# Stage 1 of a folded weight chain: six one-tap products in place of seven blocks, three middle taps evicted by VectorE, and the next stage's shared products in the same PSUM tile

## The chip, the cores and the metric

One core of one Trainium2 chip. The metric is device time in microseconds (us) of one execution. Before the change three runs gave 475.52, 476.29 and 476.63 us; the median is 476.29 us. All arithmetic is fp32.

## The reference

A residual block on `x` of shape (128 samples, 64 channels, 1024 positions). Each sample has its own style vector, and four modulated convolutions with three taps follow one another:

```
out = x
for typ in ('same', 'upsample', 'same', 'downsample'):
    s = style @ mw.T + mb                       # per sample and input channel
    weight = SCALE * w * s[:, None, :, None]    # per sample
    weight *= rsqrt(sum(weight**2 over inputs and taps) + 1e-8)
    same:       out = conv(out, weight, pad 1) + b
    upsample:   out = blur(conv_transpose(out, weight, stride 2) + b)
    downsample: out = conv(blur(out), weight, stride 2) + b
return x + out
```

There is no nonlinearity between the layers. So for each sample the four convolutions and the blurs are one linear map, and away from the ends of the row it is one short filter per pair of channels.

## The kernel before

**What it computes per group.** Samples are handled in 32 groups `q` of four. Two samples share a 128-partition tile (64 channels each), so each group has two "columns" `r` of a weight chain. For every group the kernel first multiplies the four layers' weights together, as 64x64 matrices, in three stages, and then applies the combined filter to the data.

- `scale3` (ScalarE) scales the last layer's three taps by the group's style into `wd`. With it come the sums of neighbouring taps, since `wd` is scaled from `w3x`, which holds the three taps and two sums.
- Stage 1 (`stage1`, or its two halves `stage1_a` and `stage1_b`) multiplies layer 3's taps `wd` by layer 2's taps. A product of two three-tap filters has five taps. The split version forms them from products of taps and of sums of taps, as in the multiplication of polynomials with fewer products. It writes PSUM tile `psS`. ScalarE evicts it with a scale into the SBUF tile `S` (line 399), and VectorE finishes two taps from the sums (line 481). GpSimd adds one slot (line 484).
- Stage 2 (`stage2`) multiplies the five taps `S` by the nine blurred taps `E` of the upsampling layer, into PSUM tile `psR` (line 506, or line 589 in the plain form). For groups 8 to 30 the work is shared: `share_sums` (VectorE, line 501) adds two pairs of slots of `S`, `share` multiplies these by `E` (three products, line 506), `share_copy` (ScalarE, line 529) spreads the two results over four blocks of `psR`, and `stage2_rest` adds the other products to them.
- Stage 3 multiplies by the first layer's taps (line 621) and gives the combined filter `Wf`; `combine_a` and `combine_b` form its sums `H` on VectorE (line 712).
- `conv0` to `conv4` (line 803) apply it to the data planes; each of the five is 12 matmuls of 340 columns, in three groups of four 64x64 quadrants. `output` (ScalarE, line 880) scales the results and SyncE's queue stores them.

**PSUM.** The pool `ps_w` has one buffer: two tiles `u0` and `u1`, one bank each (512 fp32 columns), one for each column `r`. `psS`, `psR` and `psW` follow one another in it. A new tile in it waits until the last reader of the old one is done. `psA` (two buffers of two banks) and `Y` (two banks, all the time) hold the results of the convolutions in columns 0 to 339. Columns from 344 on are used for small things: in `psA`, `share` puts its products there; in `Y`, the constants of the bias path.

**Order.** The schedule is written out by hand (`tc.manual_schedule()`), so every engine runs its instructions in the order of the program text, and the tile framework adds only the semaphores. In the steady state `turn_of(q)` handles the last convolutions of group `q`, the middle of group `n = q+1`, stages 2 and 3 of group `c = q+2` and stage 1 of group `s = q+4`. Its order on TensorE is `stage2(c)`, `conv2(q)`, `stage3_b`, `conv4(q)`, `stage3_a`, `conv3(n)`, `stage1_a(s)`, `conv0(q)`, `stage1_b(s)`, `share(c+1)`, sometimes a small job at the ends of the rows (`slot`), `conv1(n)`. `sharing(q)` holds for q = 5 to 27, which is 23 turns. The first turns (`early_turn`, q = 0 to 3) have the same parts in another order and no `share`. The split stage 1 runs for 28 groups, the plain `stage1` for groups 0, 1, 2 and 6.

VectorE's order around the place is: `in04` (line 790), `share_sums` (line 501), `in_g2` (line 712 on 684 columns), in most turns a small job of the bias and row-end path (`SIDE`), then the pair of line 481, then `in_g01` (line 712 on 1376 columns). ScalarE's is: `output(q, 2)`, the two evictions of `stage1_a`, `copy_m3` (line 842), `output(q, 1)`, `share_copy`, `output(q, 0)`, `scale3`.

The main line of `stage1_b` and `share` in a turn is

```
        conv0(q, *((2,) if entry else range(K)))
        ...
        outputs(q, 1)
        if s < NQ:
            stage1_b(s)
        in_g01(c)
        if sharing(q):
            share(c + 1, banks(q))
            share_copy(c + 1)
        outputs(q, 0)
        ...
        conv1(n, *((2,) if entry else range(K)))
```

Of the kernel before, what the change touches and what calls it, by code (L numbers as in the profile page):

```python
# [48 lines left out]
F32 = mybir.dt.float32  # L49
AF = mybir.ActivationFunctionType  # L50
ALU = mybir.AluOpType
# [3 lines left out]
C = 64  # L55
K = 3
# [7 lines left out]
def kernel(  # L64
# [326 lines left out]


    w3 = wio[3]
    Wq = {}
    chain = {}

# [4 lines left out]
            eng.tensor_scalar(dst, src, f, None, op0=ALU.mult)  # L401


    w3x = const.tile([P, 5, C], F32, name="w3x")
    w2n = const.tile([P, 5, C], F32, name="w2n")

    def split_weights():
        nc_g.tensor_copy(w3x[:, :K], w3)
        nc_g.tensor_scalar_mul(w2n[:, :K], woi[2], -1.0)
        for t, src in ((w3x, w3), (w2n, woi[2])):  # L410
            nc_g.tensor_add(t[:, K:], src[:, : K - 1], src[:, 1:])

    DIRECT = 3

    def scale3(q, engs=(nc_a, nc_a)):
        wd = []
        src = w3 if q < DIRECT else w3x
        n = src.shape[1]
        for j in range(2):
            t = wd_pool.tile([P, 5, C], F32, tag="wd", name=f"wd{q}_{j}")  # L420
            scaled_copy(engs[j], t[:, :n], src, tA[:, q, j : j + 1])
            wd.append(t)
        chain[q] = wd
# [17 lines left out]
    def flat(t):  # L441
        return t.rearrange("c a o -> c (a o)")

    EVEN = slice(0, K, 2)

    def stage1(q, pool=None, engs=(nc_a, nc_a), between=None):

        wd = chain[q]
        ps = unit(pool or ps_w, f"psS{q}")
        for k, (at, at1) in enumerate(((0, 3), (3, 1), (1, 4))):  # L450
            tap_matmul(ps, wd, at, 2, woi[2][:, k, :], EVEN, first=k == 0)
            tap_matmul(ps, wd, at1, 1, woi[2][:, k, :], slice(1, 2), last=k == K - 1)
        if between:
            between()
        st, _ = s_tiles(q)
        for r in range(2):
            scaled_copy(engs[r], flat(st[r][:, 1:6]), ps[r][:, : 5 * C], tB[:, q, r : r + 1])
        chain[q] = st
        return ps

    def stage1_a(q, ps=None):

        ps = ps or unit(ps_w, f"psS{q}")
        wd = chain[q]
        tap_matmul(ps, wd, 2, 2, w2n[:, 0, :], EVEN, first=True)
        tap_matmul(ps, wd, 3, 2, w2n[:, 2, :], EVEN)
        tap_matmul(ps, wd, 1, 1, w2n[:, 1, :], slice(1, 2))
        st, t = s_tiles(q)
        for r in range(2):
            scaled_copy(nc_a, flat(st[r][:, :4]), ps[r][:, C : 5 * C], tBn[:, q, r : r + 1])  # L470
        chain[q] = wd, ps, st, t

    def stage1_b(q):

        wd, ps, st, t = chain[q]
        tap_matmul(ps, wd, 2, 1, w2n[:, 3, :], slice(3, 4))
        tap_matmul(ps, wd, 4, 1, w2n[:, 4, :], slice(4, 5), last=True)
        for r in range(2):
            p1 = st[r][:, 0:1, :].to_broadcast([P, 2, C])
            sums = ps[r][:, 2 * C : 6 * C].rearrange("c (a b o) -> c a b o", a=2, b=2)[:, :, 0]  # L480
            nc_v.scalar_tensor_tensor(
                st[r][:, 4:6, :], sums, tB[:, q, r : r + 1], p1, op0=ALU.mult, op1=ALU.subtract
            )
        nc_g.tensor_add(t[:, :, 2], t[:, :, 2], t[:, :, 0])  # L484
        chain[q] = st
        whole[q] = t

    whole, shared_ps = {}, {}
    later = wsq.rearrange("c l k o -> c (l k) o")
# [8 lines left out]

    def share_sums(q):
        t = whole[q]  # L500
        nc_v.tensor_add(t[:, :, 6:8], t[:, :, 1:5:3], t[:, :, 2:6:3])

    def chain_matmul(dst, weight, st, slots, last=False):
        for r, rows in enumerate(HALF):
# [9 lines left out]

    def share(q, ps):

        at = [NB + 4 + i * C for i in range(3)]
        p12, p34 = ([b[:, i:j] for b in ps] for i, j in zip(at, at[1:]))
        chain_matmul(p12, E[:, 2], chain[q], slice(6, 7))
        chain_matmul(p34, E[:, 6], chain[q], slice(6, 7))  # L520
        chain_matmul(p34, E[:, 5], chain[q], slice(7, 8), True)
        shared_ps[q] = [b[:, at[0] : at[2]] for b in ps]

    def share_copy(q):

        ps = unit(ps_w, f"psR{q}")
        for r in range(2):
            src = shared_ps[q][r].rearrange("c (a o) -> c a o", a=2)
            nc_a.copy(  # L529
                ps[r][:, C : 5 * C].rearrange("c (a b o) -> c a b o", a=2, b=2),  # L530
                src[:, :, None, :].to_broadcast([P, 2, 2, C]),
            )
        shared_ps[q] = ps

    def stage2_rest(q):

        ps = shared_ps.pop(q)
        block = lambda i, n=1: [b[:, i * C : (i + n) * C] for b in ps]
        apart = [b[:, : 4 * C].rearrange("c (a b o) -> c a b o", a=2, b=2)[:, :, 0] for b in ps]
        plan = (  # L540
            (apart, E[:, 0], slice(1, 4, 2)),
            (block(1), Ed[:, 0], slice(2, 3)),
            (block(2), Ed[:, 1], slice(1, 2)),
            (block(3), E[:, 2], slice(3, 4)),
            (block(3), Ed[:, 2], slice(2, 3)),
            (block(4), Ed[:, 3], slice(1, 2)),
            (block(4), E[:, 4], slice(3, 4)),
            (block(5, 2), E[:, 8], slice(2, 4)),
            (block(5), E[:, 6], slice(3, 4)),
            (block(1, 2), E[:, 1], slice(4, 6)),  # L550
            (block(2), E[:, 3], slice(4, 5)),
            (block(3), Ed[:, 4], slice(5, 6)),
            (block(4), Ed[:, 5], slice(4, 5)),
            (block(5), E[:, 7], slice(5, 6)),
        )
        for n, (dst, weight, slots) in enumerate(plan):
            chain_matmul(dst, weight, chain[q], slots, n == len(plan) - 1)
        return ps
# [18 lines left out]
    def stage2_taps(q, taps, ps):  # L577

        st = chain[q]
        for n in taps:  # L580
            e = n - 2
            if e % 2 == 0:
                a, lo, m = slice(1, 4), e // 2 + 1, 3
            else:
                a, lo, m = slice(4, 6), (e + 3) // 2, 2
            for r, rows in enumerate(HALF):
                for c, cols in enumerate(HALF):
                    src = st[c if r == 0 else 1 - c]
                    nc.tensor.matmul(  # L589
                        ps[r][cols, lo * C : (lo + m) * C],  # L590
                        E[rows, e + 2, :],
                        src[rows, a, :],
                        start=(n == 0),
                        stop=(n == 8),
                        skip_group_check=True,
                    )
        return ps
# [885 lines left out]
    def turn_of(q):  # L1483
        n, c, s = q + 1, q + 2, q + 4
        entry = q == FIRST
        stage2(c)
        if entry:
            sum2(q)
            conv4(q)
            combine_a(n)  # L1490
            r_sums(c, nc_v)
        else:
            conv2(q)
            r_sums(c, nc_g)
            sum2(q)
            in2(n, nc_g)
        side(TABLES, q)
        for i in range(3):
            load(c + 1, slice(i, i + 1))
        stage3_b(c, open_a(n))  # L1500
        if entry:
            conv0(q, 0, 1)
        else:
            combine_a(n)
            conv4(q)
        stage3_a(c)
        combine_b(n)
        conv3(n)
        if entry:
            copy_m3(n)  # L1510
            stage1_a(s)
        outputs(q, 2)
        if not entry:
            if s < NQ:
                stage1_a(s)
            copy_m3(n)
        in04(n)
        if sharing(q):
            share_sums(c + 1)
        in_g2(c)  # L1520
        side(SIDE, q)
        if q in SMALL:
            l, bs = SMALL[q]
            nc_v.memset(high(bs.stop - bs.start), 0.0)
        conv0(q, *((2,) if entry else range(K)))
        if entry:
            conv1(n, 0, 1)
        outputs(q, 1)
        if s < NQ:
            stage1_b(s)  # L1530
        in_g01(c)
        if sharing(q):
            share(c + 1, banks(q))
            share_copy(c + 1)
        outputs(q, 0)
        if q in SLOTS:
            matmuls, width, rest = SLOTS[q]
            slot(matmuls, width, Y_banks)
            rest()
        if s == NQ:  # L1540
            slot(ends3, 3, unit(ps_w, "psE"), 3)
            rest3()
        conv1(n, *((2,) if entry else range(K)))
        if q in SMALL:
            small(q)
        sum1(n)
        in3(c)
        side(LATE, q)
        if s == NQ:
            in04(c)  # L1550
        in1(c, nc_g)
        if s + 1 < NQ:
            scale3(s + 1)
# [168 lines left out]
```

## Time and profile before

| | |
|---|---|
| runs | 475.52, 476.29, 476.63 us, median 476.29 |
| profiled execution | span 475.5 us from the first to the last instruction, beside 475.52 us of the fastest run shown; the page gives no other time for it |
| TensorE (PE) | busy 469.7 us, 99% |
| TensorE weight loads (PEld) | 349.5 us, 74%, beside the matmuls |
| VectorE (DVE) | 417.3 us, 88% |
| ScalarE (ACT) | 312.0 us, 66% |
| GpSimd (POOL) | 165.8 us, 35% |
| granted TensorE clock | 0.998 |

A row of the groups' view reads: line, engine, operation, tile written and tiles read, shape, count, then busy time in us and the mean duration of one in ns, then the idle time of the engine before it and what ended it. A row of the timeline reads: start and extent in us, engine, line, operation, tiles, shape and count of merged instructions; in square brackets stands the idle time just before and its releaser. Each fp32 matmul appears as two records, so a product of one 64x64 block over both columns and both halves (four quadrants) is eight records.

### The profile page before, as it was taken

What the parts mean: (1) busy time and instruction counts of PE and PEld (TensorE: products, weight loads), DVE (VectorE), ACT (ScalarE), POOL (GpSimd) and SP (SyncE); (2) the same over time, 40 slices, a digit from 0 to 9 for tenths busy, and PEclk for the clock granted to TensorE, in tenths of its full rate; (3) what the DMA queues carried; (4) which work ended last, traced back from release to release, by engine and by line L of the source; (5) the groups of instructions that cost most, each with busy time, mean ns of one, the idle gap of its engine ahead of it and who ended that gap; (6) DMA issues with size and microseconds to landing.
All of it is one profiled execution on the core that took longest, in us unless ns stands there. A gap on an engine that the chain in (4) does not pass through costs nothing.

```text
span 475.5 us, 26771 instructions
## 1 busy us (share of the span) xinstructions
PE 469.7 (99%) x11932; PEld 349.5 (74%) x11932; DVE 417.3 (88%) x694; ACT 312.0 (66%) x711; POOL 165.8 (35%) x200
## 2 busy tenths in 40 slices
PE   9999999999999999999999999999999999999996
PEld 6987788777678876677776677766788787876653
DVE  3889998879989998899979899979998999999896
ACT  4565657577766676766667666667666777766464
POOL 3634033664444342233432233422333423243200
PEclk9999999999999999999999999999999999999999
DMA  5237456535445554345544454543555544455225
GB/s 176 71 115 224 150 151 180 152 113 177 139 145 166 166 166 136 123 150 169 163 150 126 130 168 152 178 124 121 152 164 169 164 145 147 148 152 161 80 91 193
DMA packets 52707, 70.71 MB, mean 149 GB/s; under 512 B 6000, under 2 KB 50672, under 8 KB 52592
## 3 DMA queue, kind: packets, MB, share of 16 engines
q1 hardware_dynamic: 52368, 68.78, 46.3%
q8 instruction: 93, 1.52, 1.4%
q10 hardware_dynamic: 224, 0.22, 0.1%
q14 instruction: 22, 0.18, 0.1%
HBM read 35.36 MB, written 33.62 MB: 145 GB/s over the span
## 4 chain that ended last, share of the span: by engine, by line
PE 99%; DVE 0%; ACT 0%; issue 0%
PE psA L803 47%; PE Y L803 12%; PE psR L506 9%; PE psW L621 7%; PE psA L621 7%; PE psS L428 6%; PE psR L589 5%; PE psA L506 2%; PE Y L1044 2%; PE Y L183 1%; PE Y L379 1%; PE psM L220 0%; PE psE L1044 0%; PE Y L255 0%; DVE o L882 0%; PE psM L255 0%
## 5 line engine op out<-in xcount | busy, mean ns | idle before, releaser
L803 PE MATMUL psA<-T,H 64*64 64x340 f32 x2304 | 185.9, 446 | 0.0
L803 PEld LDWEIGHTS psA<-T,H 64*64 64x64 f32 x2304 | 90.7, 133 | 46.9 <-issue 2.5
L712 DVE SCALAR_TENSOR_TENSOR G<-X 128x1376 f32<-128x1376 f32 (+2 forms) x65 | 78.0, 1206 | 0.2
L776 POOL TENSOR_TENSOR T<-G 128x684 f32<-128x684 f32 x28 | 46.3, 1652 | 73.7 <-DVE G L712 73.7
L484 POOL TENSOR_TENSOR S<-S 128x128 f32<-128x128 f32 x28 | 21.6, 772 | 139.7 <-ACT S L399 139.6
L399 ACT ACTIVATE R<-psR,tC 128x448 f32<-128x448 f32 x63 | 36.6, 631 | 43.6 <-PE psR L506 25.8
L803 PE MATMUL psA<-T,Wf 64*64 64x340 f32 x768 | 63.7, 446 | 0.0
L803 PE MATMUL Y<-T,Wf 64*64 64x340 f32 x768 | 62.4, 451 | 0.0
L712 DVE SCALAR_TENSOR_TENSOR Y<-m,psA 128x340 f32<-128x340 f32 x62 | 32.0, 516 | 28.2 <-PE psA L803 26.9
L399 ACT ACTIVATE psW<-psA 128x128 f32<-128x128 f32 x100 | 19.3, 268 | 49.1 <-PE psA L621 45.0
L790 DVE TENSOR_TENSOR T<-G 128x1368 f32<-128x1368 f32 (+1 forms) x33 | 50.8, 1541 | 0.0
L399 ACT ACTIVATE Wf<-psW,t 128x256 f32<-128x256 f32 (+2 forms) x76 | 32.7, 480 | 26.7 <-PE psW L621 26.4
L761 DVE TENSOR_TENSOR T<-X 128x684 f32<-128x684 f32 x32 | 47.7, 1492 | 0.0
L506 PE MATMUL psR<-S,E 64*64 64x64 f32 (+1 forms) x1472 | 46.8, 237 | 0.0
L781 POOL TENSOR_TENSOR T<-G 128x684 f32<-128x684 f32 x28 | 46.5, 1660 | 0.0
L428 PEld LDWEIGHTS psS<-wd,w2n 64*64 64x64 f32 x1120 | 35.1, 133 | 12.9 <-issue 0.3
L506 PEld LDWEIGHTS psR<-S,E 64*64 64x64 f32 x1472 | 39.5, 134 | 4.9 <-ACT psR L529 0.2
L803 PEld LDWEIGHTS Y<-T,Wf 64*64 64x64 f32 x768 | 30.3, 132 | 16.8
L803 PEld LDWEIGHTS psA<-T,Wf 64*64 64x64 f32 x768 | 29.8, 133 | 14.5
L880 ACT ACTIVATE o<-psA,tb,td 128x340 f32<-128x340 f32 x63 | 37.1, 648 | 5.0 <-PE psA L803 2.8
L880 ACT ACTIVATE o<-y,tb,td 128x340 f32<-128x340 f32 x62 | 38.5, 678 | 0.0
L880 ACT ACTIVATE o<-Y,tb,td 128x340 f32<-128x340 f32 x62 | 36.1, 639 | 2.8 <-PE Y L803 2.0
(180 smaller groups left out, 840.4 us busy)
## 6 DMA issues: line engine op xcount, KB each, us to landing
out<-o SPq DMA_DIRECT2D x191, 170.0 KB, 2.6
X<-in_x SPq DMA_DIRECT2D x150, 172.0 KB, 3.4
X<-in_x SPq DMA_DIRECT2D x14, 516.0 KB, 5.0
par<-in_params SPq DMA_DIRECT2D x3, 192.0 KB, 3.8
Xe<-in_x_ends SPq DMA_DIRECT2D x1, 512.0 KB, 4.5
out<-Oe SPq DMA_DIRECT2D x2, 96.0 KB, 2.1
out<-o ACTq DMA_DIRECT2D x1, 170.0 KB, 2.8
par<-in_params SPq DMA_DIRECT2D x1, 160.0 KB, 2.7
```

The source lines that it names most:

```text
L399: nc_a.activation(dst, src, AF.Copy, scale=f)
L428: nc.tensor.matmul(ps[r][cols, at * C : (at + n) * C], weight[rows], wd[c if r == 0 else 1 - c][rows, taps], start=first, stop=last, skip_ ...
L506: nc.tensor.matmul(dst[r][cols], weight[rows], st[c if r == 0 else 1 - c][rows, slots, :], start=False, stop=last, skip_group_check=True,)
L589: nc.tensor.matmul(ps[r][cols, lo * C : (lo + m) * C], E[rows, e + 2, :], src[rows, a, :], start=(n == 0), stop=(n == 8), skip_group_check ...
L621: nc.tensor.matmul(dst[r][cols], weight[rows], t[rows, c, slots, :], start=first, stop=last, skip_group_check=True,)
L712: nc_v.scalar_tensor_tensor(out, x, f, y, op0=ALU.mult, op1=op)
L761: nc_v.tensor_sub(t[:, pairs, 0, :NJ], plane(X, 3, pairs), plane(X, 1, pairs))
L776: eng.tensor_add(t[:, :, 0, :NJ], plane(g, 2), plane(g, 1))
L781: eng.tensor_sub(t[:, :, 1, :NJ], plane(g, 2), plane(g, 1))
L790: nc_v.tensor_sub(t[:, pairs, :, :NJ], both(a, PL), both(b, 1))
L803: nc.tensor.matmul(ps[s][cols, :NB], w, Ts[q, tag][rows, c, i, g : g + NB], start=(g == 0 and (m == 3 or alone)), stop=(g == K - 1), skip_ ...
L880: nc_a.activation(dst, src, AF.Identity, bias=add, scale=d3)
```

## The change

Stage 1 now keeps six kinds of taps in `w3x` and `w2n`: the three taps, the two neighbouring sums and the sum of the two outer taps. Each is multiplied with its counterpart once, in six products of one 64-column block each: three in `stage1_a` (outer taps into blocks 1 and 3, middle tap into block 2) and three in `stage1_b` added onto the same blocks. Before, `stage1_a` had two products of two blocks and one of one block, and `stage1_b` two of one block.

`stage1_a` now has four ScalarE evictions in place of two: the two end taps (slots 0 and 4 of `S`), and the middle product twice (slots 5 and 7). GpSimd's addition, now slot 6 from slots 0 and 4, moves from the end of `stage1_b` to the end of `stage1_a`. In `stage1_b` VectorE evicts three taps at once (192 columns where it was 128), subtracting slots 5 to 7, which ScalarE and GpSimd wrote. The taps lie in slots 0 to 4 in order, and so the slots that stage 2 reads are renumbered; their number and sizes are the same.

`share` no longer writes to columns 344 on of `psA`. It writes to blocks 4 and 7 of the tile `psS` of group `s`, which `stage1_b` returns, and the copies to blocks 1 to 4 stay within that tile, which then serves as `psR`. No new tile is taken for `psR`.

The plain `stage1` has three products of three blocks each in place of three of two and three of one. `scale3` scales six blocks in place of five from group 3 on. `split_weights` (GpSimd, once) has seven instructions in place of four.

```diff
-    w3x = const.tile([P, 5, C], F32, name="w3x")
-    w2n = const.tile([P, 5, C], F32, name="w2n")
+    w3x = const.tile([P, 6, C], F32, name="w3x")
+    w2n = const.tile([P, 6, C], F32, name="w2n")
 
     def split_weights():
         nc_g.tensor_copy(w3x[:, :K], w3)
-        nc_g.tensor_scalar_mul(w2n[:, :K], woi[2], -1.0)
+        nc_g.tensor_scalar_mul(w2n[:, EVEN], woi[2][:, EVEN], -1.0)
+        nc_g.tensor_copy(w2n[:, 1:2], woi[2][:, 1:2])
         for t, src in ((w3x, w3), (w2n, woi[2])):
-            nc_g.tensor_add(t[:, K:], src[:, : K - 1], src[:, 1:])
+            nc_g.tensor_add(t[:, K : K + 2], src[:, : K - 1], src[:, 1:])
+            nc_g.tensor_add(t[:, K + 2], src[:, 0], src[:, 2])
...
-            t = wd_pool.tile([P, 5, C], F32, tag="wd", name=f"wd{q}_{j}")
+            t = wd_pool.tile([P, 6, C], F32, tag="wd", name=f"wd{q}_{j}")
...
     def stage1(q, pool=None, engs=(nc_a, nc_a), between=None):
...
-        for k, (at, at1) in enumerate(((0, 3), (3, 1), (1, 4))):
-            tap_matmul(ps, wd, at, 2, woi[2][:, k, :], EVEN, first=k == 0)
-            tap_matmul(ps, wd, at1, 1, woi[2][:, k, :], slice(1, 2), last=k == K - 1)
+        for k in range(K):
+            tap_matmul(ps, wd, k, K, woi[2][:, k, :], slice(0, K), first=k == 0, last=k == K - 1)
...
     def stage1_a(q, ps=None):
...
-        tap_matmul(ps, wd, 2, 2, w2n[:, 0, :], EVEN, first=True)
-        tap_matmul(ps, wd, 3, 2, w2n[:, 2, :], EVEN)
-        tap_matmul(ps, wd, 1, 1, w2n[:, 1, :], slice(1, 2))
+        for n, i in enumerate((0, 2, 1)):
+            tap_matmul(ps, wd, i + 1, 1, w2n[:, i, :], slice(i, i + 1), first=n == 0)
         st, t = s_tiles(q)
         for r in range(2):
-            scaled_copy(nc_a, flat(st[r][:, :4]), ps[r][:, C : 5 * C], tBn[:, q, r : r + 1])
+            ends = ps[r][:, C : 5 * C].rearrange("c (a b o) -> c a b o", a=2, b=2)[:, :, 0]
+            scaled_copy(nc_a, st[r][:, 0:5:4, :], ends, tBn[:, q, r : r + 1])
+        for r in range(2):
+            middle = ps[r][:, None, 2 * C : 3 * C].to_broadcast([P, 2, C])
+            scaled_copy(nc_a, st[r][:, 5:8:2, :], middle, tB[:, q, r : r + 1])
+        nc_g.tensor_add(t[:, :, 6], t[:, :, 0], t[:, :, 4])
         chain[q] = wd, ps, st, t
 
     def stage1_b(q):
 
         wd, ps, st, t = chain[q]
-        tap_matmul(ps, wd, 2, 1, w2n[:, 3, :], slice(3, 4))
-        tap_matmul(ps, wd, 4, 1, w2n[:, 4, :], slice(4, 5), last=True)
+        for n, (at, i) in enumerate(((1, 3), (3, 4), (2, 5))):
+            tap_matmul(ps, wd, at, 1, w2n[:, i, :], slice(i, i + 1), last=n == K - 1)
         for r in range(2):
-            p1 = st[r][:, 0:1, :].to_broadcast([P, 2, C])
-            sums = ps[r][:, 2 * C : 6 * C].rearrange("c (a b o) -> c a b o", a=2, b=2)[:, :, 0]
             nc_v.scalar_tensor_tensor(
-                st[r][:, 4:6, :], sums, tB[:, q, r : r + 1], p1, op0=ALU.mult, op1=ALU.subtract
+                flat(st[r][:, 1:4]),
+                ps[r][:, C : 4 * C],
+                tB[:, q, r : r + 1],
+                flat(st[r][:, 5:8]),
+                op0=ALU.mult,
+                op1=ALU.subtract,
             )
-        nc_g.tensor_add(t[:, :, 2], t[:, :, 2], t[:, :, 0])
         chain[q] = st
         whole[q] = t
+        return ps
...
     def share_sums(q):
         t = whole[q]
-        nc_v.tensor_add(t[:, :, 6:8], t[:, :, 1:5:3], t[:, :, 2:6:3])
+        nc_v.tensor_add(t[:, :, 5:7], t[:, :, 0:2], t[:, :, 2:4])
...
     def share(q, ps):
 
-        at = [NB + 4 + i * C for i in range(3)]
-        p12, p34 = ([b[:, i:j] for b in ps] for i, j in zip(at, at[1:]))
-        chain_matmul(p12, E[:, 2], chain[q], slice(6, 7))
-        chain_matmul(p34, E[:, 6], chain[q], slice(6, 7))
-        chain_matmul(p34, E[:, 5], chain[q], slice(7, 8), True)
-        shared_ps[q] = [b[:, at[0] : at[2]] for b in ps]
-
-    def share_copy(q):
-
-        ps = unit(ps_w, f"psR{q}")
-        for r in range(2):
-            src = shared_ps[q][r].rearrange("c (a o) -> c a o", a=2)
+        p12, p34 = ([b[:, i * C : (i + 1) * C] for b in ps] for i in (4, 7))
+        chain_matmul(p12, E[:, 2], chain[q], slice(5, 6))
+        chain_matmul(p34, E[:, 6], chain[q], slice(5, 6))
+        chain_matmul(p34, E[:, 5], chain[q], slice(6, 7), True)
+        for b in ps:
+            src = b[:, 2 * C : 8 * C].rearrange("c (a b o) -> c a b o", a=2, b=3)[:, :, 2]
             nc_a.copy(
-                ps[r][:, C : 5 * C].rearrange("c (a b o) -> c a b o", a=2, b=2),
+                b[:, C : 5 * C].rearrange("c (a b o) -> c a b o", a=2, b=2),
                 src[:, :, None, :].to_broadcast([P, 2, 2, C]),
             )
         shared_ps[q] = ps
...
         if s < NQ:
-            stage1_b(s)
+            psS = stage1_b(s)
         in_g01(c)
         if sharing(q):
-            share(c + 1, banks(q))
-            share_copy(c + 1)
+            share(c + 1, psS)
```

More of the change, by code (lines that the diff above doesn't have):

```diff
@@ L393 @@
     w3 = wio[3]
+    EVEN = slice(0, K, 2)
     Wq = {}
@@ L442, in flat @@
         return t.rearrange("c a o -> c (a o)")
-    EVEN = slice(0, K, 2)
     def stage1(q, pool=None, engs=(nc_a, nc_a), between=None):
@@ L456, in stage1 @@
         for r in range(2):
-            scaled_copy(engs[r], flat(st[r][:, 1:6]), ps[r][:, : 5 * C], tB[:, q, r : r + 1])
+            scaled_copy(engs[r], flat(st[r][:, :5]), ps[r][:, : 5 * C], tB[:, q, r : r + 1])
         chain[q] = st
@@ L540, in stage2_rest @@
         plan = (
-            (apart, E[:, 0], slice(1, 4, 2)),
+            (apart, E[:, 0], slice(0, 5, 4)),
             (block(1), Ed[:, 0], slice(2, 3)),
-            (block(2), Ed[:, 1], slice(1, 2)),
-            (block(3), E[:, 2], slice(3, 4)),
+            (block(2), Ed[:, 1], slice(0, 1)),
+            (block(3), E[:, 2], slice(4, 5)),
             (block(3), Ed[:, 2], slice(2, 3)),
[L546 to L554, printed above, removed]
+            (block(4), Ed[:, 3], slice(0, 1)),
+            (block(4), E[:, 4], slice(4, 5)),
+            (block(5, 2), E[:, 8], slice(2, 5, 2)),
+            (block(5), E[:, 6], slice(4, 5)),
+            (block(1, 2), E[:, 1], slice(1, 4, 2)),
+            (block(2), E[:, 3], slice(1, 2)),
+            (block(3), Ed[:, 4], slice(3, 4)),
+            (block(4), Ed[:, 5], slice(1, 2)),
+            (block(5), E[:, 7], slice(3, 4)),
         )
@@ L582, in stage2_taps @@
             if e % 2 == 0:
-                a, lo, m = slice(1, 4), e // 2 + 1, 3
+                a, lo, m = slice(0, 5, 2), e // 2 + 1, 3
             else:
-                a, lo, m = slice(4, 6), (e + 3) // 2, 2
+                a, lo, m = slice(1, 4, 2), (e + 3) // 2, 2
             for r, rows in enumerate(HALF):
```

## The prediction

> **What bounds the kernel now.** I read the page first: its busy shares, the clock row and the chain that ended last.
>
> ```profile
> span 475.5 us, 26771 instructions
> PE 469.7 (99%) x11932; PEld 349.5 (74%) x11932; DVE 417.3 (88%) x694; ACT 312.0 (66%) x711; POOL 165.8 (35%) x200
> PEclk9999999999999999999999999999999999999999
> PE 99%; DVE 0%; ACT 0%; issue 0%
> ```
>
> TensorE is busy for 99% of the span at full granted clock, and the chain that ended last is TensorE alone. So two things count: time that a TensorE product takes, and any new place where TensorE has to wait. An instruction on another engine costs nothing until TensorE waits for it.
>
> Then I read the timeline of one steady turn (q = 20) around the change.
>
> ```profile
> 327.34 0.73 PE L428 MATMUL psS<-wd,w2n 64*64 64x128 f32 x24
> 327.89 1.90 PE L803 MATMUL psA<-T,Wf 64*64 64x340 f32 x24
> 328.10 0.84 ACT L399 ACTIVATE S<-psS,tBn 128x256 f32<-128x256 f32 x2 [0.32 <-PE psS L428]
> ...
> 329.02 0.82 POOL L484 TENSOR_TENSOR S<-S 128x128 f32<-128x128 f32 x1 [5.16 <-ACT S L399]
> ...
> 329.45 0.94 DVE L1123 TENSOR_TENSOR Ve<-Ve,c 128x512 f32<-128x512 f32 x1
> 329.61 0.41 PE L428 MATMUL psS<-wd,w2n 64*64 64x64 f32 x16
> 329.84 0.53 PE L506 MATMUL psA<-S,E 64*64 64x64 f32 x24
> 330.19 1.90 PE L803 MATMUL psA<-T,H 64*64 64x340 f32 x24
> 330.32 0.60 DVE L481 SCALAR_TENSOR_TENSOR S<-psS,tB,S 128x128 f32<-128x128 f32 x2
> 330.74 0.63 ACT L529 COPY psR<-psA 128x256 f32<-128x256 f32 x2
> ...
> 331.90 0.40 PE L506 MATMUL psR<-S,E 64*64 64x128 f32 x8
> ```
>
> Read the starts, since matmul extents overlap. `stage1_a` at 327.34, `conv0` at 327.89, `stage1_b` at 329.61, `share` at 329.84, `conv1` at 330.19, the next turn's stage 2 at 331.90: no gap. The pair L481, which reads `psS`, runs from 330.32 to 330.92, long after `share` has started. Before the change this hurts nobody, since `share` writes into `psA` and only ScalarE's L529 waits for L481. Stage 2 follows L529 0.5 us later.
>
> **The change part by part.**
>
> *1. Seven blocks to six (gain).* `stage1_b` has two one-block products between 329.61 and 329.84, so one costs 0.115 us. `stage1_a` has two products of two blocks and one of one block in 0.55 us, so a two-block product costs (0.55 - 0.115) / 2 = 0.217 us, 1.9 times one block. Before: 0.55 + 0.23 = 0.78 us; after: 6 x 0.115 = 0.69 us. `stage1_a` gets shorter by 0.205 us and `stage1_b` longer by 0.115: 0.09 us less per group, all on TensorE's path. With 28 groups this is -2.5 us. The four plain `stage1` move from 9 blocks to 9 blocks: nothing.
>
> The Trainium skill, "TensorEngine Tiling (Array Packing)", section Instruction Overhead, puts some 60 cycles of fixed cost on each matmul. As an estimate from that page a two-block product would cost (60 + 128) / (60 + 64) = 1.5 blocks, and six single ones as much as the five before, so that this gain would vanish and the sum be 2.5 us higher. The trace has 1.9, and the measurement decides.
>
> *2. `share` moves into the tile that L481 reads (loss).* The first question is whether an access to other columns of the same bank has to wait. `share` writes blocks 4 and 7, L481 reads blocks 1 to 3. The trace shows one such pair, in the timeline of turn 4: VectorE's memset of `Y` from column 344 on against ScalarE's reads of `Y` columns 0 to 339.
>
> ```profile
> 99.47 1.17 ACT L880 ACTIVATE o<-Y,tb,td 128x340 f32<-128x340 f32 x2
> ...
> 100.74 0.14 DVE L1524 MEMSET Y<- 128x96 f32 x1 [2.39 <-ACT o L880]
> ```
>
> The columns are disjoint, and still VectorE stood idle for 2.39 us and started 0.10 us after the second read ended (99.47 + 1.17 = 100.64). The program orders accesses by bank, not by column. So `share` will wait for L481, and everything behind it on TensorE (slots, `conv1`, the next turn) waits too, as TensorE runs in the order written.
>
> The Trainium skill says the same by rule: "PSUM — Partial Sum Buffer", section PSUM bank collisions raise a hardware error, has two engines collide in one bank and quadrant even at different columns, and asks for semaphores by bank and quadrant rather than by address. By that rule the wait below is due; by address the sum would be the first rival's. The trace agrees, with the 2.39 us above.
>
> The price per turn needs durations by form, two more turns, and one place where TensorE already waits for VectorE.
>
> ```profile
> L712 DVE SCALAR_TENSOR_TENSOR Y<-m,psA 128x340 f32<-128x340 f32 x62 | 32.0, 516 | 28.2 <-PE psA L803 26.9
> L399 ACT ACTIVATE wd<-w3x,tA 128x320 f32<-128x320 f32 x58 | 29.6, 574 | 0.0
> L399 ACT ACTIVATE S<-psS,tBn 128x256 f32<-128x256 f32 x56 | 23.5, 471 | 11.6 <-PE psS L428 11.6
> L399 ACT ACTIVATE psW<-psA 128x128 f32<-128x128 f32 x100 | 19.3, 268 | 49.1 <-PE psA L621 45.0 <-issue 4.1
> L481 DVE SCALAR_TENSOR_TENSOR S<-psS,tB,S 128x128 f32<-128x128 f32 x56 | 16.7, 339 | 2.6 <-PE psS L428 1.3 <-ACT o L880 1.0
> L529 ACT COPY psR<-psA 128x256 f32<-128x256 f32 x46 | 14.7, 362 | 1.7 <-DVE S L481 1.0
> ```
>
> ```profile
> 299.45 0.53 PE L506 MATMUL psA<-S,E 64*64 64x64 f32 x24
> 300.48 0.61 DVE L481 SCALAR_TENSOR_TENSOR S<-psS,tB,S 128x128 f32<-128x128 f32 x2
> 301.33 0.41 PEld L506 LDWEIGHTS psR<-S,E 64*64 64x64 f32 x6 [0.23 <-ACT psR L529]
> 301.51 0.42 PE L506 MATMUL psR<-S,E 64*64 64x128 f32 x6
> ...
> 313.40 0.53 PE L506 MATMUL psA<-S,E 64*64 64x64 f32 x24
> 313.69 0.61 DVE L481 SCALAR_TENSOR_TENSOR S<-psS,tB,S 128x128 f32<-128x128 f32 x2 [0.62 <-ACT o L880]
> ```
>
> ```profile
> 321.97 1.07 DVE L712 SCALAR_TENSOR_TENSOR Y<-m,psA 128x340 f32<-128x340 f32 x2 [1.93 <-PE psA L803]
> ...
> 323.09 1.95 PE L803 MATMUL Y<-T,Wf 64*64 64x340 f32 x24
> ```
>
> L481 grows from 128 to 192 columns: by the slope between 339 ns at 128 and 516 at 340, 0.83 ns a column, it takes 392 ns, and the pair 0.60 + 0.11 = 0.71 us. TensorE goes on 0.05 us after VectorE is done (323.04 to 323.09). In turn 20 the pair starts at 330.32, held by L1123 in VectorE's queue, ends at 331.03, and TensorE could write at 331.08. It stands at `share` from 329.84 - 0.09 = 329.75 on, since stage 1 got shorter while VectorE's work before L481 did not change. That is 1.33 us, of which 0.06 comes back, since the half product over column 0 needs only the first of the pair: 1.27 us, with nothing to cover it.
>
> How far other turns differ is in the second fence. In the turn of 313.40 VectorE was free, and the pair started 0.29 us after `share`, which is TensorE's own latency: 0.29 + 0.71 + 0.05 - 0.06 = 0.99 us, the lower end. In the turn of 299.45 four small jobs stood ahead and it was 1.03 us: 1.03 + 0.09 + 0.70 = 1.82 us, the upper end. Turn 20, at 0.48, lies where most turns do, and I take it for all. L529's 46 copies are two per turn, so 23 turns: 23 x 1.27 = +29.2 us. If the wait sits on the weight load rather than on the matmul, 0.18 us more is lost per turn (301.33 to 301.51, the one restart of that kind); I take none.
>
> *3. The copy within the tile.* It now starts after `share` and not only after L481. From `share`'s start stage 2 is 2.06 us away (329.84 to 331.90, `conv1` between). `share` needs 0.53 us and the copies 0.63, with two starts of at most 0.1 in all 1.36. Hidden behind `conv1` by 0.7 us; without that cover it would cost 1.0 us a turn. `output(q, 0)` comes later by the stall, as does TensorE's next need of `psA`. Freeing columns 344 on of `psA` removes no wait.
>
> *4. ScalarE.* Four evictions of 128 columns for two of 256. Their start-to-start time lies between 0.17 us (four L399 copies of 128 columns at 268 ns in 0.77 us) and the 0.37 us of the 256-column pair (0.84 - 0.47). At 0.27, midway, and with the 0.10 us by which such a copy outlasts its successor's start (0.47 - 0.37), the four take 4 x 0.27 + 0.10 = 1.18 us, 0.34 more. They begin 0.21 us after `conv0` starts and must be done when `stage1_b` starts, 1.72 us after it: free by 0.3. At 0.37 they would make `stage1_b` late by 0.12 us. `scale3` grows by 64 of 320 columns, about 0.05 us twice a turn; `stage1_a` needs it most of a turn later. `copy_m3` is 0.34 us later and is read after `conv1`.
>
> *5. GpSimd ahead of L481.* Its sum was behind L481 and is now a new wait of L481. From `conv0`'s start: two evictions done at 0.85, start 0.08 later, 0.82 us of work, 0.10 to VectorE as for the memset: 1.85 us. L481's data come off TensorE at 1.72 + 0.35 + 0.29 = 2.36. Free by 0.5 us. Later jobs of its queue move none ahead.
>
> *6. Set-up.* Three more small GpSimd instructions, once, in front of idle time of up to 8.5 us that the view of waits shows:
>
> ```profile
> POOL tb L332 <- DVE oc L977: 13.8, 2, 8.5
> ```
>
> Nothing. In the first turns L481, longer by 0.1 us a pair, holds the next `psR` in five cases: 0.5 us at most, left out. No DMA moves.
>
> **The sum.** -2.5 + 29.2 = +26.7 us on a profiled execution of 475.5 us gives 502.2. The median of the runs lies 0.8 us above that execution, so 503.0 us.
>
> **The rivals.**
>
> *No wait (faster).* If the order went by columns, or if L481 were over in time, only part 1 would be left: 476.3 - 2.5 = 473.8 us. For it: no row shows TensorE itself held by a read in other columns. Against it: the memset, and that L481 starts at the earliest 0.29 us after `share`. It decides if `share` starts within 0.1 us of `stage1_b`'s last product.
>
> *A later chain through ScalarE and GpSimd.* GpSimd's sum can be slow:
>
> ```profile
> 142.83 1.62 POOL L484 TENSOR_TENSOR S<-S 128x128 f32<-128x128 f32 x1
> ```
>
> With this and 256-column prices for the evictions L481 could begin at 1.05 + 0.08 + 1.62 + 0.10 = 2.85 us after `conv0` against 2.63 in a turn like turn 20 (330.32 less 327.69), and `stage1_b` is 0.12 late: 0.34 x 23 = +7.8, 510.8 us. Against it: 0.82 us in the turn shown.
>
> *Six products are no cheaper than five*, a fixed cost per product being hidden in my 1.9: 505.5 us.
>
> **Numbers.** Chances: forecast 0.79, no wait 0.06, late chain 0.08, no gain from products 0.05, a measured nothing 0.02. Range: the low end is every turn like that of 313.40, 476.3 - 2.5 + 23 x 0.99 = 496.6; the high end is 1.27 + 0.18 in each turn and no gain, 476.3 + 33.4 = 509.7, and the late chain at 510.8: 496 to 511. The runs shown spread over 0.23%, so changes within 0.2% are no change: faster 0.06, same 0.02, slower 0.92.
>
> **What would show it.** Right: in the 23 turns `share` (L506 onto `psS`) starts about 0.05 us after L481's first and second, TensorE idles about 1.2 us there, its busy share falls to some 94%, and VectorE's L481 appears in the chain that ended last; `stage1_a` to `conv0` is 0.35 us, `stage1_b` to `share`'s place 0.35. Wrong: no gap before `share`; or L481 released by GpSimd L484; or gaps elsewhere, such as before `stage1_b` or stage 2.

## The result

The changed kernel takes 506.78 us (median of 506.24 to 507.56) against 476.01 us before, a ratio of 1.064 with a 95% interval of 1.063 to 1.066: 30.8 us slower. 503.0 us had been forecast, in a range of 496 to 511.

The page of the changed kernel has these lines for the ones shown of before:

```profile
span 505.3 us, 27107 instructions
...
PE 480.2 (95%) x12060; PEld 368.6 (73%) x12060; DVE 405.1 (80%) x694; ACT 324.1 (64%) x767; POOL 158.1 (31%) x203
...
PEclk9999999999999999999999999999999999999999
```

TensorE is no longer busy all the time: 25.1 us of the span are idle, where it was 5.8 us. The clock is untouched. Where the idle time lies is told by the view of waits:

```profile
PEld psS L513 <- DVE S L483: 22.5, 23, 1.5
...
ACT psS L530 <- PE psS L513: 19.5, 23, 1.4
PE psS L513 <- DVE S L483: 19.4, 23, 1.4
```

L513 is the helper that `share` calls, and L483 is VectorE's pair, L481 before. TensorE waits 23 times, once in each turn with sharing, always for that pair. No wait of `share` stood in the view of before. The same turn as in the prediction, in the timeline of the changed kernel:

```profile
347.37 0.53 PE L431 MATMUL psS<-wd,w2n 64*64 64x64 f32 x24
...
347.72 1.90 PE L804 MATMUL psA<-T,Wf 64*64 64x340 f32 x24
347.93 0.62 ACT L400 ACTIVATE S<-psS,tBn 128x128 f32<-128x128 f32 x2
...
348.44 0.63 ACT L400 ACTIVATE S<-psS,tB 128x128 f32<-128x128 f32 x2
348.63 0.45 POOL L474 TENSOR_TENSOR S<-S 128x128 f32<-128x128 f32 x1 [4.79 <-ACT S L400]
348.68 1.13 DVE L713 SCALAR_TENSOR_TENSOR G<-X 128x684 f32<-128x684 f32 x1
...
349.43 0.53 PE L431 MATMUL psS<-wd,w2n 64*64 64x64 f32 x24
...
349.74 0.68 DVE L1124 TENSOR_TENSOR Ve<-Ve,c 128x512 f32<-128x512 f32 x1
350.34 0.73 DVE L483 SCALAR_TENSOR_TENSOR S<-psS,tB,S 128x192 f32<-128x192 f32 x2
...
350.80 0.83 PE L513 MATMUL psS<-S,E 64*64 64x64 f32 x22 [0.84 <-DVE S L483]
...
351.42 0.46 PE L804 MATMUL psA<-T,H 64*64 64x340 f32 x2
...
351.65 0.63 ACT L530 COPY psS<-psS 128x256 f32<-128x256 f32 x2 [0.84 <-PE psS L513]
...
353.14 0.48 PE L513 MATMUL psS<-S,E 64*64 64x128 f32 x7
```

`stage1_b` starts at 349.43 and takes 0.345 us of TensorE's time, but `share` starts at 350.80, 0.06 us after the first instruction of the pair has ended (350.34 + 0.40), and can finish only after the second; `conv1` starts at 351.42. From `conv0` to `conv1` it is now 3.70 us, where it was 2.30 (327.89 to 330.19).

To see the whole, I took the first start of each part of TensorE's order from the trace, turn by turn, and averaged over the 23 turns (the first begins at 106.97 us before and 108.12 after, at `conv4`; the last ends at 434.4 and 464.3):

| from this part's start to the next one's | before, us | after, us | 23 turns, us |
|---|---|---|---|
| `stage1_a` | 0.551 | 0.347 | -4.7 |
| `stage1_b`, with the wait behind it | 0.231 | 1.369 | +26.2 |
| `share`, with the wait inside it | 0.350 | 0.620 | +6.2 |
| all nine others together | 13.10 | 13.15 | +1.1 |
| a turn | 14.24 | 15.49 | +28.8 |

The six products take 0.347 + 0.347 us where the five took 0.551 + 0.231: 0.088 us less, 2.0 us in these turns. The wait is 1.369 - 0.347 = 1.02 us ahead of `share` and 0.27 us inside it, 1.29 us a turn, 29.7 us in all. From turn to turn it lies between 1.07 and 1.83 us.

### The profile page after: what moved, and what is told of

Its sections match the earlier page's. It is cut to its first block, busy times and chain, and to the rows that moved or that the text cites. A ratio compares the mean times of both kernels' runs of the same rounds, so it can differ in the third digit from the quotient of the medians.

```text
span 505.3 us, 27107 instructions
## 1 busy us (share of the span) xinstructions
PE 480.2 (95%) x12060; PEld 368.6 (73%) x12060; DVE 405.1 (80%) x694; ACT 324.1 (64%) x767; POOL 158.1 (31%) x203
## 5 line engine op out<-in xcount | busy, mean ns | idle before, releaser
L804 PE MATMUL psA<-T,H 64*64 64x340 f32 x2304 | 189.4, 446 | 0.1
L804 PEld LDWEIGHTS psA<-T,H 64*64 64x64 f32 x2304 | 106.4, 133 | 34.7 <-issue 2.4
L513 PE MATMUL psS<-S,E 64*64 64x64 f32 (+1 forms) x2024 | 71.1, 235 | 19.4 <-DVE S L483 19.4
L713 DVE SCALAR_TENSOR_TENSOR G<-X 128x1376 f32<-128x1376 f32 (+2 forms) x65 | 84.3, 1303 | 0.2
L513 PEld LDWEIGHTS psS<-S,E 64*64 64x64 f32 x2024 | 61.2, 134 | 27.3 <-DVE S L483 22.5
L713 DVE SCALAR_TENSOR_TENSOR Y<-m,psA 128x340 f32<-128x340 f32 x62 | 32.0, 516 | 48.2 <-PE psA L804 47.0
L474 POOL TENSOR_TENSOR S<-S 128x128 f32<-128x128 f32 x28 | 12.8, 456 | 135.1 <-ACT S L400 135.1
L400 ACT ACTIVATE psW<-psA 128x128 f32<-128x128 f32 x100 | 19.4, 269 | 49.6 <-PE psA L622 45.3
L400 ACT ACTIVATE R<-psS,tC 128x448 f32<-128x448 f32 x46 | 26.7, 630 | 32.8 <-PE psS L513 32.8
L713 DVE SCALAR_TENSOR_TENSOR y<-psA,m 128x680 f32<-128x680 f32 x31 | 26.9, 866 | 24.0 <-PE psA L804 21.6
L804 PEld LDWEIGHTS Y<-T,Wf 64*64 64x64 f32 x768 | 28.6, 132 | 18.2
L431 PEld LDWEIGHTS psS<-wd,w2n 64*64 64x64 f32 x1344 | 31.7, 134 | 13.4
```

The lines of the kernel that those rows point to most:

```text
L400: nc_a.activation(dst, src, AF.Copy, scale=f)
L431: nc.tensor.matmul(ps[r][cols, at * C : (at + n) * C], weight[rows], wd[c if r == 0 else 1 - c][rows, taps], start=first, stop=last, skip_ ...
L474: nc_g.tensor_add(t[:, :, 6], t[:, :, 0], t[:, :, 4])
L513: nc.tensor.matmul(dst[r][cols], weight[rows], st[c if r == 0 else 1 - c][rows, slots, :], start=False, stop=last, skip_group_check=True,)
L713: nc_v.scalar_tensor_tensor(out, x, f, y, op0=ALU.mult, op1=op)
L804: nc.tensor.matmul(ps[s][cols, :NB], w, Ts[q, tag][rows, c, i, g : g + NB], start=(g == 0 and (m == 3 or alone)), stop=(g == K - 1), skip_ ...
```

## The experiments

The theory: `share` now writes the PSUM bank that the pair reads, though in other columns, so the program makes TensorE wait for the end of the pair, and nothing covers it. Its rivals: the time goes to another part of the change (ScalarE's four evictions, GpSimd's sum ahead of the pair, the wider pair), or the products are not cheaper.

**1. The shared products back in `psA`.**

```diff
-    def share(q, ps):
+    def share(q, ps, banks_a):
...
-        p12, p34 = ([b[:, i * C : (i + 1) * C] for b in ps] for i in (4, 7))
+        at = [NB + 4 + i * C for i in range(3)]
+        p12, p34 = ([b[:, i:j] for b in banks_a] for i, j in zip(at, at[1:]))
...
-        for b in ps:
-            src = b[:, 2 * C : 8 * C].rearrange("c (a b o) -> c a b o", a=2, b=3)[:, :, 2]
+        for b, ba in zip(ps, banks_a):
+            src = ba[:, at[0] : at[2]].rearrange("c (a o) -> c a o", a=2)
...
-            share(c + 1, psS)
+            share(c + 1, psS, banks(q))
```

> The changed kernel with one thing undone: the shared products go to psA, columns 344 on, as before; stage 1 with six products and the wider eviction stay, and the copies still go to blocks 1 to 4 of the S tile. If TensorE waits because share writes the bank that L481 reads: no gap ahead of share, each turn 0.09 us shorter than before the change, so 476.0 - 2.5 = 473.5 us (0.5 us more if the longer eviction costs something in the first turns). If the gap came from anything else in the change (four evictions, GpSimd ahead of L481, the longer L481): still about 506 us. If six products of one block are no cheaper than the five before: 476.0 us.

475.03 us against 476.02, ratio 0.998 (0.997 to 1.000). In its timeline the gap is gone, with the same pair on VectorE:

```profile
328.89 0.53 PE L431 MATMUL psS<-wd,w2n 64*64 64x64 f32 x24
...
329.24 0.53 PE L513 MATMUL psA<-S,E 64*64 64x64 f32 x24
...
329.59 1.90 PE L805 MATMUL psA<-T,H 64*64 64x340 f32 x24
329.80 0.73 DVE L483 SCALAR_TENSOR_TENSOR S<-psS,tB,S 128x192 f32<-128x192 f32 x2
```

So it is the write into the tile that the pair reads, though in other columns, that makes the wait. Each of these tiles fills one bank, so no run here tells an order by tile from an order by bank. Four evictions, GpSimd's sum and the wider pair are all still there and cost TensorE next to nothing. The gain is smaller than the 2.5 us expected. Stage 1 gives its 2.0 us in the 23 turns, as in the changed kernel. But stage 2 then begins late or is held in a few turns, 0.67 us in all, and further small waits take 0.4 us: the turns are 0.9 us shorter together.

**2. VectorE's small jobs behind the pair.**

```diff
-        side(SIDE, q)
-        if q in SMALL:
-            l, bs = SMALL[q]
-            nc_v.memset(high(bs.stop - bs.start), 0.0)
         conv0(q, *((2,) if entry else range(K)))
...
             psS = stage1_b(s)
+        side(SIDE, q)
+        if q in SMALL:
+            l, bs = SMALL[q]
+            nc_v.memset(high(bs.stop - bs.start), 0.0)
         in_g01(c)
```

> The changed kernel, with VectorE's small jobs of the bias and row-end path queued behind the pair of L483 and not ahead of it. If share waits for the end of the pair, the pair now starts in every turn as early as TensorE's data allow, as in the two turns where no small job stood ahead: share starts 1.14 us after stage1_b's first product and not 1.37, so 23 x 0.22 = 5 us less, 501.7 us. If share waits for something else than that pair (ScalarE's or GpSimd's work): 506.8 us.

502.17 us, ratio 1.056 (1.053 to 1.058). The view of waits of this kernel:

```profile
PE psS L513 <- DVE S L483: 14.5, 23, 1.0
```

The wait shrinks by 4.9 us, from 19.4 to 14.5, with the pair's start, and the time by 4.6.

**3. The pair made late.**

```diff
+    scratch = const.tile([P, 256], F32, name="scratch")
+    nc_v.memset(scratch, 0.0)
...
+            if sharing(q):
+                nc_v.tensor_add(scratch, scratch, scratch)
             psS = stage1_b(s)
```

> The changed kernel with one more VectorE instruction (128x256, about 0.42 us as L508 of that size) queued straight ahead of the pair in the 23 turns. If the pair's end sets when TensorE goes on, all of it lands on the path, but for 0.3 us in the two turns where VectorE was free: 23 x 0.42 - 0.6 = +9.1 us, 515.9 us. If VectorE has slack there: 506.8 us.

511.92 us, ratio 1.078 (1.074 to 1.081): 5.1 us more than the changed kernel, not 9.1. A row of the waits, then the place in the timeline:

```profile
PE psS L513 <- DVE S L483: 25.5, 23, 1.7
```

```profile
352.86 0.41 DVE L1534 TENSOR_TENSOR scratch<-scratch 128x256 f32<-128x256 f32 x1
353.19 0.73 DVE L483 SCALAR_TENSOR_TENSOR S<-psS,tB,S 128x192 f32<-128x192 f32 x2
```

The wait grows by 6.1 us (25.5 - 19.4). The expectation was wrong in its size: an instruction of 0.41 us holds the next one up by 0.33 only (352.86 to 353.19), since neighbours on VectorE overlap. 21 x 0.33 would be 6.9. That added time lands on TensorE confirms the theory; that it does so at 0.29 us a turn is what the starts say (1.656 us from `stage1_b` to `share` against 1.369). Together the 23 turns grew by 6.9 us (356.2 to 363.1). What lies outside them was 1.7 us shorter in this trace (147.4 against 149.1), all of it ahead of the first turn with sharing (106.42 us against 108.12), so that the span grew by 5.2 only.

**4. `share` between the groups of `conv1`.**

```diff
-        if sharing(q):
-            share(c + 1, psS)
         outputs(q, 0)
...
-        conv1(n, *((2,) if entry else range(K)))
+        if sharing(q):
+            conv1(n, 0, 1)
+            share(c + 1, psS)
+            conv1(n, 2)
+        else:
+            conv1(n, *((2,) if entry else range(K)))
```

> The changed kernel with share issued between the second and the third group of conv1, and output(q, 0) ahead of the copies on ScalarE. If the wait is for the pair only, two groups (1.15 us) cover most of the 1.29 us, some 0.2 us stay. But stage 2 then comes 0.92 us after share starts, and share with the copies needs 0.53 + 0.63 + two starts = 1.3 us: 0.4 us of new wait on ScalarE. 23 x (1.29 - 0.6) = 16 us less: 490.8 us. If the wait is not for the pair, no gain.

491.08 us, ratio 1.032 (1.029 to 1.035), as expected. Its waits:

```profile
PEld psS L513 <- ACT psS L530: 11.1, 21, 0.7
...
PEld psS L513 <- DVE S L483: 4.9, 14, 0.9
...
PE psS L513 <- DVE S L483: 0.3, 1, 0.3
```

The wait for the pair is nearly covered, and a wait of stage 2 for ScalarE's copies takes its place, 0.5 us in 21 turns. By these numbers no place for `share` between the end of the pair and stage 2 is free of both: the pair ends 1.64 us after `stage1_b` starts, stage 2 begins 0.345 + 0.35 + 1.72 = 2.41 us after it, and `share` with the copies needs some 1.3 by the estimate above.

**5 and 6. A version to beat both.** The first experiment leaves out the copied sum in block 4, which no product of its `psS` had written. So it was tried whole, and with VectorE's order changed once more.

```diff
+    Zb = const.tile([P, C], mybir.dt.bfloat16, name="Zb")
+    nc_g.memset(Zb, 0.0)
...
+        for r, rows in enumerate(HALF):
+            for cols in HALF:
+                nc.tensor.matmul(
+                    ps[r][cols, 4 * C : 5 * C],
+                    Zb[rows],
+                    Zb[rows],
+                    start=False,
+                    stop=False,
+                    skip_group_check=True,
+                )
```

> As the first experiment (shared products in psA, six products), with one product of 64 columns of bf16 zeros per group added to stage1_a, which writes block 4 of the S tile so that the copy into it is added to and not overwritten. The first experiment left the copied sum out of block 4 of R, and its time is that of the same instructions. If a bf16 product costs a quarter of an fp32 one (0.115 / 4 = 0.03 us), 28 x 0.03 = 0.8 us come on top of its 475.0 us: 475.8 us, no change against before. If it costs a full one, 28 x 0.115 = 3.2 us: 478.2 us.

476.52 us against 475.64, ratio 1.002 (1.000 to 1.004): no gain is left. Its timeline:

```profile
327.55 0.53 PE L433 MATMUL psS<-wd,w2n 64*64 64x64 f32 x24
...
327.89 0.21 PE L471 MATMUL psS<-Zb 64*64 64x64 bf16 x4
...
327.92 1.93 PE L817 MATMUL psA<-T,Wf 64*64 64x340 f32 x24
```

The zeros delay `conv0` by 0.03 us, and by the starts `conv0` itself takes 1.745 us where it took 1.718: 0.054 us a group, not 0.03 and not 0.115. It lies between the two cases expected. `share` follows `stage1_b` after 0.35 us, as in the first experiment, so the gap stays away with every product in place.

```diff
-        side(SIDE, q)
-        if q in SMALL:
-            l, bs = SMALL[q]
-            nc_v.memset(high(bs.stop - bs.start), 0.0)
...
             psS = stage1_b(s)
+        if q in SMALL:
+            side(SIDE, q)
+            l, bs = SMALL[q]
+            nc_v.memset(high(bs.stop - bs.start), 0.0)
         in_g01(c)
+        if q not in SMALL:
+            side(SIDE, q)
```

> As the one before, with VectorE's small jobs of the row ends queued behind in_g01, so that the pair of L483 is never late. In the first experiment stage 2 was late in five turns by 0.11 to 0.23 us, 0.67 us in all, against before; if that comes from the late pair, it goes: 475.1 us. If in_g01 or the jobs themselves are then late for something else: 476 us or more.

485.29 us, ratio 1.019 (1.016 to 1.022): the second branch, and far beyond it. With the jobs behind `in_g01`, `sum1` (VectorE's L726, which reads the convolution's result in `psA`) is late and TensorE waits for it:

```profile
PE psA L817 <- DVE y L726: 4.4, 5, 2.0
```

Stage 2 and the parts after it lose 8 us against the fifth, in some of the turns. Some 1.7 us of that is an estimate for a slower clock and no wait: right behind the longest of these waits (1.95 us, up to 311.98) the granted clock was 0.73 from 312 to 314 us, 0.50 to 316 and 0.91 to 318, which is (0.27 + 0.50 + 0.09) x 2 us of full clock lost. Behind the waits of up to 1.4 us in the changed kernel, and of 1.7 in the third experiment, the clock stayed at 1.00. One place does not show that the wait brought the slower clock on. Whether the 0.67 us of the first experiment come from the late pair stays open, since this run moved more than that. No complete version beat the kernel before.

## Why the prediction was right

**The wait for the pair (step 2).** Right in mechanism, place, count and size. 23 turns; 1.29 us a turn against 1.27 taken, 29.7 us against 29.2. TensorE goes on 0.05 to 0.06 us after each instruction of the pair (0.05 was taken from the conv4 row), and the wait sits on the matmul, without the 0.18 us of a late weight load. The pair takes 0.73 us where 0.71 was worked out. The wait of turn 20, taken for all turns, is 1.29 us here and so is the mean, while single turns reach from 1.07 to 1.83 (0.99 to 1.82 were the ends given); that one turn hits the mean so closely is in part luck. One row on a memset in turn 4 carried the wait itself, and the first experiment shows that it was read rightly: the order does not go by column.

**Seven blocks to six (step 1).** 0.088 us a group against 0.09. The estimate worked out from the Trainium skill, "TensorEngine Tiling (Array Packing)", section Instruction Overhead, that the gain would vanish, does not hold here: 64-column products follow one another at 0.115 us, and six of them are shorter than the five before.

**ScalarE and GpSimd (steps 4 and 5).** Free, as worked out: the four evictions end 1.35 us after `conv0` starts (347.72 to 349.07; 1.39 by the estimate, 0.21 + 1.18), and GpSimd's sum ends 1.36 us after it (1.75 by the estimate, since it took 0.45 us and not 0.82). The late chain, a rival, did not come.

**The copy within the tile (step 3).** Hidden, as said: the copies end at 352.28, 0.86 us ahead of stage 2 at 353.14.

**The rest of the distance.** The measured difference is 30.8 us and the sum was 26.7. In the span it is 29.8 us: 29.7 of waits (29.2 in the sum), less 2.0 of products in the 23 turns (2.5 in the sum, for 28 groups), 1.1 in the nine other parts, which the sum put at nothing and whose cause was not followed up, and 1.0 outside these turns. The last is mostly the start: the first turn with sharing begins at 108.12 us here, at 106.97 before and at 106.42 to 107.36 in the first four experiments, which have the changed kernel's code up to there but for one memset in the third; so it is most likely scatter from run to run and not the change. One more microsecond is an error of accounting. The execution profiled after the change took 507.07 us at a span of 505.3; three experiments have 1.8 us outside the span as well (476.07 at 474.3, 501.74 at 500.0, 512.28 at 510.5). So the profiled execution of before, span 475.5, presumably took some 477.3 us and lay above its median, and the prediction, which found nothing for it but the 475.52 us of the fastest run, took it as lying 0.8 us below.

**What was said to show.** The gap is there; TensorE's busy share is 95% (94% said). L483 does stand in the chain that ended last, but that chain goes back only to 424 us in this trace, so its shares say little; the view of waits is the one that carries the reading.

## What to carry to other kernels

A PSUM tile that is still to be evicted is no free space: before placing new products beside old ones, look which engine reads that bank and when it is done, since here the program ordered each one-bank tile as a whole. On an engine that is busy for 99%, a gain of 0.09 us a turn is small beside one new wait of 1.29; list for each moved write who reads its new bank last. And the cover of a late reader is what stands between it and the next write: here `conv1` had covered the pair, and the new order put `share` on the wrong side of it.

## What was not expected of the hardware

VectorE does more work after the change and is busy for less time, 405.1 us against 417.3. The reason lies mainly in one line, `in3`, an addition of two SBUF tensors (L761 before, L762 after). The timeline of before, then of the changed kernel:

```profile
328.67 0.87 DVE L712 SCALAR_TENSOR_TENSOR G<-X 128x684 f32<-128x684 f32 x1
...
332.58 1.66 POOL L776 TENSOR_TENSOR T<-G 128x684 f32<-128x684 f32 x1 [2.74 <-DVE G L712]
...
333.11 1.85 DVE L761 TENSOR_TENSOR T<-X 128x684 f32<-128x684 f32 x1
```

```profile
352.74 1.66 POOL L777 TENSOR_TENSOR T<-G 128x684 f32<-128x684 f32 x1 [3.65 <-DVE G L713]
...
354.31 0.86 DVE L762 TENSOR_TENSOR T<-X 128x684 f32<-128x684 f32 x1
```

Beside GpSimd's instruction it takes 1.85 us and ends some 0.7 us after it (334.96 against 334.24). Started 0.09 us before GpSimd's ends, it takes 0.86. The stall moved it past most of GpSimd's work, and its mean over 32 fell from 1492 ns to 920. In these rows the one that starts second pays: before, GpSimd's sum (329.02) started behind VectorE's L712 (328.67) and took 0.82 us; after, it started first (348.63 against 348.68), took 0.45, and VectorE's L713 took 1.13 us instead of 0.87. The Trainium skill, "SBUF — State Buffer", section Who interferes with whom, describes this as a port pair that VectorE and GpSimd share as an exclusive lock, where the order of issue decides who blocks; these rows agree. For the time of this kernel it changed nothing, as VectorE was not what TensorE waited for at that place.

The other surprise is the bf16 product of the fifth experiment: 0.054 us for 64 columns in four quadrants, half of it as a longer `conv0` behind it, where an fp32 one takes 0.115.
